# Layer 3's feed-forward weights made inside layer 2's feed-forward loop

## The chip, the cores and the metric

The kernel runs on one core of one Trainium2 chip. The core has five engines with a queue each: TensorE (PE in the profile; its weight loads, PEld, overlap the matmuls), VectorE (DVE), ScalarE (ACT), GpSimd (POOL) and SyncE (SP), which here only issues transfers. An engine works through its queue in order; semaphores tie the queues together. The metric is device microseconds of one launch. Before the change the median of 10 runs is 2324.54 us (2320.92 to 2329.66).

## The reference, cut to what matters

Four layers follow each other on x of shape (4, 256, 256), each a cross attention to a context of 1601 rows and a feed-forward part. The change touches the feed-forward part of layer 2, where each token goes to one of four experts, and that of layer 3, whose weights are first rounded to -1, 0 or 1:

```python
def _quant_weight(w):
    scale = jnp.mean(jnp.abs(w)) + EPS
    wq = jnp.clip(jnp.round(w / scale), -1.0, 1.0)
    return (wq, scale)
...
gate = jax.nn.silu(_qlinear(x, w_gate))
up = _qlinear(x, w_up)
return _qlinear(gate * up, w_down)
```

`_qlinear(x, w)` rounds its input too, multiplies by the rounded weight and scales the product back. The three weights are 256 x 1024 numbers each. Rounded weights and scales depend on nothing but the inputs of the kernel.

Layer 2's feed-forward part is

```python
probs = softmax(x @ Wr + br); top_w, top_idx = top_k(probs, 1)
y = (silu(x @ Wg[e]) * (x @ Wu[e])) @ Wd[e]      # e = top_idx of the token
out = y * top_w
```

and layer 3's attention has 32 heads of 8, with normalised queries and keys.

## The kernel before

**Order.** A framework puts the instructions of each engine in order by a cost model of its own, so a line can run well before or after its place in the program. An instruction given to `pin` keeps the program's order among the pinned ones of its engine. Matmuls made with `mm`, and transposes handed to `ordered`, are pinned while `self.strict` is set. In layer 3's main loop every instruction is pinned.

**Layer 2's feed-forward part** (`l2_ffn`, L992). The router sorts the 1024 tokens by expert into NS = 11 tiles of 128 rows, each tile for one expert. Eleven indirect transfers on POOL's queue (L1154) gather the rows `f2xr`, through three buffers; the first can start when `f2src` is there. The hidden width 1024 is cut into NC = 4 chunks. The loop at L1204 goes over 44 pairs of chunk and tile, in 46 steps s, three stages deep: `gated` (L1173: four matmuls `f2gu`, Silu on ScalarE, product `f2h` on DVE), `turned` (L1182: two transposes `f2tph`, copied by ScalarE to `f2hT`) and `down` (L1190: matmuls `f2y`, added by DVE to `f2acc`). During the first 11 steps `brought` (L1166) transposes the next gathered tile into `f2xsT`, with an eviction by ScalarE and DVE in turn. The profile shows a float32 matmul as two.

**Early work for layer 3.** `l3_early` (L1839) makes keys and values of layer 3's first batch, a tile of 128 context rows at a time: four matmuls into one bank (`f2fill`), two copies by ScalarE, squares and their sums for every two tiles. There are NM = 13 such tiles, and `fill(n)` takes n steps of the generator. Eight steps are taken ahead of the loop (L1068, L1093, L1160), the others in steps 10 to 15 and 39 to 43 (L1209 to L1212). Behind the last tile the generator loads the next batch's context on SP's queue, takes the root of the sums (L1864) and goes through the keys in eight parts: POOL scales a part (L1918) and splits it with DVE (L1968, L1969), DVE transposes it (L1922), SP stores it (L1930, `kd<-kt`).

Behind the loop POOL gathers the results (L1225). Layer 3 starts with 11 tiles of batch 1 (`fill`), between which lie the first batch's normalisation, transposes, the copy `xT` (L2048) and the queries.

**Layer 3** (`l3`, L1985). The main loop at L2334 goes over 4 batches, 4 groups of heads and 13 tiles of keys. A step has eight score matmuls `s`, two exponentials of 128x1024 on ScalarE (`e`), and the matmuls `o` of the step before. After each group DVE copies `o` to `os`. Between steps `slot` (L2287) deals pieces of other streams: keys and values of later batches, queries, and from the second batch on the feed-forward part of the batch before. A piece tells its cost in advance, or asks for the one spare bank of PSUM by `yield True`.

One of these streams is `weights` (L2074), dealt in the first batch only. For each of the three weights it issues two transfers of 512 KB on POOL's queue, sums absolute values with DVE (two of 128x1024), adds the partitions up by a matmul with ones, makes scale and reciprocal, and rounds in three passes of DVE over each half. `half` (L2280), the feed-forward part of a finished batch, waits until all three weights are there.

Of the kernel before, what the change touches and what calls it, by code (L numbers as in the profile page):

```python
# [11 lines left out]
F32 = mybir.dt.float32  # L12
# [85 lines left out]
class Kernel:  # L98
# [893 lines left out]
    def l2_ffn(self, other):  # L992
# [13 lines left out]
        with ExitStack() as es:  # L1006
# [152 lines left out]
            chunks.append(load(1))  # L1159
            fill(3)  # L1160
            self.strict = False
            expert = []
# [3 lines left out]
            def brought(n):  # L1166
                tp = ps.tile([P, 2, P], F32, name="f2tpx", tag="tp")
                for k in range(2):
                    nc.tensor.transpose(tp[:, k, :], xr[n][:, k * P : (k + 1) * P], self.ident)
                self.evac(xsT[:, n], tp)  # L1170
                expert.append(nc.tensor.value_load(ei[:, n : n + 1], min_val=0, max_val=E2 - 1))
# [29 lines left out]
            work = [(c, n) for c in range(NC) for n in range(NS)]  # L1201
            hs, hTs = {}, {}
            brought(0)
            for s in range(len(work) + 2):  # L1204
                if s < len(work):
                    hs[s] = gated(*work[s])
                    if s + 1 < NS:
                        brought(s + 1)
                    elif s < NS + 5:  # L1209
                        fill(1)  # L1210
                    elif s >= len(work) - 5:
                        fill(1)  # L1212
                if 0 <= s - 1 < len(work):
                    hTs[s - 1] = turned(hs.pop(s - 1))
                if s >= 2:
                    down(*work[s - 2], hTs.pop(s - 2))
                    c, n = work[s - 2]
                    if n == NS - 1 and c + 2 < NC:
                        chunks.append(load(c + 2))
            self.back = []  # L1220
            for t in range(8):
# [592 lines left out]
    def values3(self, pool):  # L1814
# [7 lines left out]
        return va  # L1822

    def l3_begin(self, b, st):
        st["kr"] = self.a3.tile([P, NM, D], F32, name="kr3")
# [159 lines left out]
    def l3(self, first):  # L1985
# [10 lines left out]
        with ExitStack() as es:  # L1996
# [7 lines left out]
            self.va3.append(self.values3(self.late3))  # L2004
            wq, ws = {}, {}

# [27 lines left out]
            def queries(b, st, fill=lambda n: None):  # L2034
# [37 lines left out]
                yield 0.0  # L2072

            def weights():  # L2074

                for name, n in (("l3_wg", 2), ("l3_wu", 2), ("l3_wd", 8)):
                    v = i[name].rearrange("(k p) e -> p k e", p=P)
                    w = []
                    for c in range(2):
                        w.append(two.tile([P, I3], F32, name="wf3", tag="g3"))  # L2080
                        nc.gpsimd.dma_start(
                            w[c].rearrange("p (k e) -> p k e", k=n // 2), v[:, c * n // 2 : (c + 1) * n // 2]
                        )
                    for _ in range(2):
                        yield 0.0
                    sm = self.small.tile([P, 2], F32, name="wsum")
                    for c in range(2):
                        yield 1.2
                        nc.vector.tensor_reduce(sm[:, c : c + 1], w[c], AX.X, ALU.add, apply_absolute_value=True)
                    yield 0.0  # L2090
                    yield True
                    tot = bank()[:, 0:2]
                    self.mm(tot, self.ones, sm, True, True)
                    s = one.tile([P, 1], F32, name=name + "s")
                    r = self.small.tile([P, 1], F32, name="wrec")
                    nc.vector.tensor_reduce(s, tot, AX.X, ALU.add)
                    nc.vector.tensor_scalar(s, s, 1.0 / (I3 * D), 1e-5, ALU.mult, ALU.add)
                    nc.vector.reciprocal(r, s)
                    wb = one.tile([P, n, 2048 // n], BF16, name=name + "b")
                    wr = wb.rearrange("p k e -> p (k e)")  # L2100
                    for c in range(2):
                        yield 0.8
                        nc.vector.tensor_scalar(w[c], w[c], r, RND, ALU.mult, ALU.add)
                        yield 0.7
                        nc.vector.tensor_scalar(w[c], w[c], RND, 1.0, ALU.subtract, ALU.min)
                        yield 0.7
                        nc.vector.tensor_scalar(wr[:, c * I3 : (c + 1) * I3], w[c], -1.0, None, ALU.max)
                    wq[name], ws[name] = wb, s
                    yield 0.0

# [376 lines left out]
    def run(self):  # L2487
# [23 lines left out]
        self.l2_xattn()  # L2511
        with ExitStack() as es:
            self.l3_open(es)
            first = {}
# [127 lines left out]
```

## Time and profile before

| | |
|---|---|
| median of 10 runs | 2324.54 us |
| the profiled execution | 2321.94 us, its span 2319.9 us |
| granted TensorE clock, mean | 0.987 |
| layer 2's feed-forward loop, first `f2gu` to last `f2y` | 1673.4 to 1814.3 us |
| layer 3's first exponential; last | 1838.4; 2290.6 us |
| first batch of layer 3, first exponential to the second batch's first | 1838.4 to about 1958.7 us |
| ScalarE's waits for `s` in 1836 to 1960 us | 21.7 us |
| busy share of the span: PE, DVE, ACT, POOL | 96%, 63%, 55%, 41% |

All times inside the program are microseconds from the start of the span of one profiled execution. In a timeline a row has the start, the time it took, the engine, the line, the operation with the tiles written and read, the count, and in brackets how long the engine had been idle and what ended that. In layer 3 all lines are L77, a helper that pins, so rows are told apart by tiles. Buffer numbers are left out of names: `wf` is the tile `wf3`, `f2gu` stands for all of its buffers.

### The profile page before, as it was taken

The page shows a single profiled execution, that of the slowest core. Times are in us where ns is not written, and L with a number is a line of the kernel's source. Part 1 is how long each engine was busy: PE and PEld are TensorE (multiplying, and loading weights), DVE is VectorE, ACT ScalarE, POOL GpSimd, SP SyncE. Part 2 cuts the span into 40 slices and gives each one's busy share as a digit, 9 for nine tenths or more (in the row PEclk, how much of TensorE's full clock was granted, in tenths as well). Part 3 has the DMA queues.
Part 4 walks back from the last instruction along what each step waited for, and adds up shares of the span by engine and source line. Part 5 has one row for each costly group of instructions (what it writes and reads, how often), then busy time and mean ns, then how long its engine had stood idle before and what let it go on. Part 6 is the DMA issues. An engine that isn't in the chain of part 4 may idle for free.

```text
span 2319.9 us, 42336 instructions
## 1 busy us (share of the span) xinstructions
PE 2233.8 (96%) x14379; PEld 1375.8 (59%) x14379; DVE 1467.2 (63%) x3534; ACT 1276.4 (55%) x2884; POOL 953.1 (41%) x1716
## 2 busy tenths in 40 slices
PE   8989999999989999999999999999999989999997
PEld 5677988867745555555555555555765633443332
DVE  5543645953567777887787778777334575748343
ACT  3334546633665555544555555554332587888996
POOL 2014655612445554555445545554221354334220
PEclk9999999989999999999999999999999999999999
DMA  7155687833721111111111111100534453434220
GB/s 275 43 187 167 187 161 211 264 100 98 230 87 40 52 53 53 57 53 36 50 48 53 53 53 53 57 2 10 200 125 121 138 150 107 103 95 110 79 68 18
DMA packets 157166, 234.47 MB, mean 101 GB/s; under 512 B 33993, under 2 KB 122825, under 8 KB 155754
## 3 DMA queue, kind: packets, MB, share of 16 engines
q1 hardware_dynamic: 140902, 190.86, 25.5%
q0 software_dynamic: 11280, 31.60, 5.9%
q10 hardware_dynamic: 4772, 9.31, 1.3%
q8 instruction: 118, 1.93, 0.3%
q14 instruction: 94, 0.77, 0.1%
HBM read 169.94 MB, written 61.74 MB: 100 GB/s over the span
## 4 chain that ended last, share of the span: by engine, by line
PE 82%; DVE 8%; DMA 4%; ACT 2%; issue 2%; POOL 1%; SPq 0%; ACTq 0%; DVEq 0%; POOLq 0%
PE o L117 18%; PE s L117 17%; PE o L77 7%; PE b L77 4%; PE f2gu L117 3%; PE s L77 3%; PE f1gu L117 3%; PE fill L1328 2%; PE acc L117 2%; PE f0gu L117 2%; PE tpq L117 2%; PE av L117 2%; DMA f0xr<-f0xd,f0src 2%; PE f0y L117 2%; PE f2y L117 1%
## 5 line engine op out<-in xcount | busy, mean ns | idle before, releaser
L1593 ACT ACTIVATE p<-s,nmsm 128x448 f32<-128x448 f32 (+2 forms) x512 | 324.7, 639 | 388.0 <-DVE nmsm L1588 315.7
L117 PE MATMUL o<-pT,va 128*128 128x256 f32 (+2 forms) x1920 | 431.2, 377 | 0.8 <-DVE pT L1637 0.3
L117 PE MATMUL s<-kT,qT 128*32 128x448 f32 (+2 forms) x4096 | 423.7, 550 | 4.2 <-ACT p L1593 4.2
L77 ACT ACTIVATE e<-s 128x1024 f32<-128x1024 f32 (+1 forms) x416 | 393.0, 1040 | 51.8 <-PE s L77 50.5
L117 PEld LDWEIGHTS o<-pT,va 128*128 128x128 f32 (+1 forms) x1920 | 344.4, 190 | 124.9 <-issue 72.5
L1631 POOL TENSOR_SCALAR p<-p,rm 128x416 f32<-128x416 f32 x508 | 318.3, 650 | 6.3
L1588 DVE TENSOR_REDUCE nmsm<-s 128x1 f32<-128x448 f32 (+4 forms) x384 | 292.8, 783 | 4.2
L1637 DVE STREAM_TRANSPOSE pT<-p 128x448 f32<-128x448 f32 (+4 forms) x384 | 277.8, 777 | 10.3 <-POOL p L1631 10.3
L117 PEld LDWEIGHTS s<-kT,qT 128*32 128x32 f32 x4096 | 121.7, 109 | 249.7 <-issue 213.1
L77 PE MATMUL o<-e,va 128*32 128x512 f32 (+1 forms) x1664 | 247.8, 609 | 5.2 <-DVE os L77 5.1
L1621 POOL TENSOR_TENSOR rm<-em,tot 32x8 f32<-32x8 f32 x256 | 50.3, 196 | 336.3 <-DVE tot L1618 304.0
L1585 DVE TENSOR_TENSOR s<-s,mask 128x64 f32<-128x64 f32 (+4 forms) x384 | 92.2, 259 | 123.8 <-PE s L117 77.8
L77 PEld LDWEIGHTS s<-qb,kb 32*128 32x128 f32 (+1 forms) x1664 | 64.8, 179 | 175.3 <-issue 130.8
L526 POOL DMA_INDIRECT f0xr<-f0xd,f0src x95 | 91.8, 966 | 58.8 <-PE f0tph L583 47.8
L77 PE MATMUL s<-qb,kb 32*128 32x256 f32 (+1 forms) x1664 | 110.3, 329 | 4.0 <-ACT e L77 1.3
L1328 PE MATMUL fill<-wkc_early,ctxT 128*128 128x256 f32 (+1 forms) x444 | 107.6, 393 | 6.7 <-ACT va_early L1336 4.5
L1593 ACT ACTIVATION_READ_ACCUMULATOR p<-s,nmsm 128x1 f32 x512 | 100.5, 196 | 0.0
L77 POOL CAST kb<-kf 128x384 fp32r<-128x384 f32 (+1 forms) x126 | 64.8, 543 | 86.7 <-PE s L77 35.2
L1328 PEld LDWEIGHTS fill<-wkc_early,ctxT 128*128 128x128 f32 (+1 forms) x444 | 85.1, 195 | 22.0 <-ACT va_early L1336 5.6
L117 PE MATMUL f2gu<-f2wgu,f2xsT 128*128 x176 | 84.7, 605 | 0.6 <-ACT f2xsT L114 0.3
L634 POOL DMA_INDIRECT f0yt<-f0yd,f0slot x64 | 68.1, 1064 | 35.0 <-DMA kd<-kT_early 15.8
L77 PEld LDWEIGHTS o<-e,va 128*32 128x32 f32 (+1 forms) x1664 | 41.4, 108 | 68.7 <-issue 35.1
(565 smaller groups left out, 3661.6 us busy)
## 6 DMA issues: line engine op xcount, KB each, us to landing
kf<-kd SPq DMA_DIRECT2D x384, 48.0 KB
vd<-va_early SPq DMA_DIRECT2D x96, 128.0 KB
kd<-kT_early SPq DMA_DIRECT2D x48, 256.0 KB
kT<-kd SPq DMA_DIRECT2D x16, 768.0 KB
va<-vd SPq DMA_DIRECT2D x16, 768.0 KB
kd<-kt SPq DMA_DIRECT2D x96, 128.0 KB
f0yd<-f0ys SPq DMA_DIRECT2D x95, 128.0 KB
ctxT<-in_ctxT SPq DMA_DIRECT2D x5, 1664.0 KB
```

The lines of the kernel that those rows point to most:

```text
L77: ins = f(*a, **kw)
L117: self.ordered(self.nc.tensor.matmul(out, lhsT, rhs, start=start, stop=stop, **kw))
L526: nc.gpsimd.indirect_dma_start(out=t, out_offset=None, in_=xd[:, :], in_offset=bass.IndirectOffsetOnAxis(ap=src[:, n : n + 1], axis=0),)
L634: nc.gpsimd.indirect_dma_start(out=yt, out_offset=None, in_=yd[:, :], in_offset=bass.IndirectOffsetOnAxis(ap=slot[:, t, r : r + 1], axis=0),)
L1328: ins = nc.tensor.matmul(tp[:rows, t, :], ctxT[u // NKV2][:, k, c0 : c0 + rows], w[u % NKV2][:, k, :], start=k == 0, stop=k == 1,)
L1585: nc.vector.tensor_tensor(sv, sv, mask[:, e0:e1, : nt - CT, :].rearrange("p n t i -> p n (t i)"), ALU.add)
L1588: nc.vector.tensor_reduce(ms[:, 0, e0:e1], s[:, n0:n1, : nt * 32], AX.X, ALU.max, negate=True)
L1593: nc.scalar.activation(p[:, n, : nt * 32], s[:, n, : nt * 32], AF.Exp, bias=ms[:, 0, e : e + 1], accum_out=ms[:, 1, e : e + 1],)
L1621: nc.gpsimd.tensor_tensor(r[32 * a : 32 * a + 32], e[:, a], tot, ALU.mult)
L1631: nc.gpsimd.tensor_scalar(p[:, n, : nt * 32], p[:, n, : nt * 32], r[:, e : e + 1], 1.0, ALU.mult, ALU.mult)
L1637: self.pin(nc.vector.transpose(pT[:, 2 * c + n0 : 2 * c + n1, :nt, :].rearrange("p n t i -> p n (t i)"), p[:, n0:n1, : nt * 32],))
```

## The change

`weights` leaves layer 3 and becomes `l3_weights`, a generator called in layer 2's feed-forward loop at the end of each step from step 10 on, and run out behind the loop. The sums of absolute values become activations on ScalarE, four of 128x512 for each weight, and the roundings go to GpSimd. Its instructions on ScalarE, DVE and GpSimd are pinned. Rounded weights and scales lie in a pool of their own, open until the end of layer 3, the loaded weights in a pool of layer 2's part. `half` no longer waits for weights.

Apart from that, `fill(3)` ahead of the loop becomes `fill(4)`, one further `fill(1)` lies behind the first `brought`, the order of PE stays pinned until step 1, the transposes of `brought` are pinned as long as that holds, and the first batch's `xT` is copied by ScalarE.

```diff
-            fill(3)
-            self.strict = False
+            fill(4)
...
+            wf = es.enter_context(tc.tile_pool(name="f2wf", bufs=2))
+            small = self.l3_weights(wf, self.take)
             brought(0)
+            fill(1)
             for s in range(len(work) + 2):
+                if s == 1:
+                    self.strict = False
...
+                if s >= 10:
+                    next(small, None)
+            for _ in small:
+                pass
...
+    def l3_weights(self, pool, bank):
+        nc = self.nc
+        self.wb3, self.ws3 = {}, {}
+        self.w3 = self.es3.enter_context(self.tc.tile_pool(name="w3", bufs=1, side="right"))
+        for name, n in (("l3_wg", 2), ("l3_wu", 2), ("l3_wd", 8)):
+            v = self.i[name].rearrange("(k p) e -> p k e", p=P)
+            w = []
+            for c in range(2):
+                w.append(pool.tile([P, I3], F32, name="wf3", bufs=2))
+                nc.gpsimd.dma_start(w[c].rearrange("p (k e) -> p k e", k=n // 2), v[:, c * n // 2 : (c + 1) * n // 2])
+            for _ in range(3):
+                yield
+            sm = pool.tile([P, 4], F32, name="wsum", bufs=1)
+            for c in range(4):
+                junk = pool.tile([P, 512], F32, name="wjunk", bufs=1)
+                h = slice(c % 2 * 512, c % 2 * 512 + 512)
+                self.pin(nc.scalar.activation(junk, w[c // 2][:, h], AF.Abs, accum_out=sm[:, c : c + 1]))
+                yield
+            yield
+            tot = bank()[:, 0:4]
+            self.ordered(nc.tensor.matmul(tot, self.ones, sm, start=True, stop=True))
+            s = self.ws3[name] = self.w3.tile([P, 1], F32, name=name + "s")
+            r = self.small.tile([P, 1], F32, name="wrec")
+            self.pin(nc.vector.tensor_reduce(s, tot, AX.X, ALU.add))
+            self.pin(nc.vector.tensor_scalar(s, s, 1.0 / (I3 * D), 1e-5, ALU.mult, ALU.add))
+            self.pin(nc.vector.reciprocal(r, s))
+            wb = self.wb3[name] = self.w3.tile([P, n, 2048 // n], BF16, name=name + "b")
+            wr = wb.rearrange("p k e -> p (k e)")
+            for c in range(2):
+                yield
+                self.pin(nc.gpsimd.tensor_scalar(w[c], w[c], r, RND, ALU.mult, ALU.add))
+                yield
+                self.pin(nc.gpsimd.tensor_scalar(w[c], w[c], RND, 1.0, ALU.subtract, ALU.min))
+                self.pin(nc.gpsimd.tensor_scalar(wr[:, c * I3 : (c + 1) * I3], w[c], -1.0, None, ALU.max))
...
-            wq, ws = {}, {}
+            wq, ws = self.wb3, self.ws3
...
-                nc.vector.tensor_copy(xT, tp.rearrange("p k q t -> p k (q t)"))
+                (nc.vector.tensor_copy if b else nc.scalar.copy)(xT, tp.rearrange("p k q t -> p k (q t)"))
...
-            def weights():
...
-                while len(wq) < 3 or "xn" not in states[b]:
+                while "xn" not in states[b]:
...
-                    streams = [t for t in streams if t.left] if b else [Stream(weights(), 3)]
+                    streams = [t for t in streams if t.left] if b else []
```

More of the change, by code (lines that the diff above doesn't have):

```diff
@@ L1168, in brought @@
                 for k in range(2):
-                    nc.tensor.transpose(tp[:, k, :], xr[n][:, k * P : (k + 1) * P], self.ident)
+                    self.ordered(nc.tensor.transpose(tp[:, k, :], xr[n][:, k * P : (k + 1) * P], self.ident))
                 self.evac(xsT[:, n], tp)
@@ L2072, in queries @@
                 yield 0.0
-            def weights():
[L2076 to L2109, printed above, removed]
             def scale_of(v, name):
@@ L2512, in run @@
         with ExitStack() as es:
+            self.es3 = es
             self.l3_open(es)
```

## The prediction

> **What bounds the kernel now.** I read the page first (TensorE, "PE", is busy 96% of the span), then the table of windows over layer 2's feed-forward loop (1673 to 1815 us) and the start of layer 3 (1838 to 1965 us), then the timeline of the places where a window sags. Columns of a window: its length, busy time and count of PE, weight load, DVE, ACT and POOL, granted clock, DMA share, GB/s.
>
> ```profile
> 1665.00:1673.00 8.00, 4.02 (x18) 2.70 (x16) 1.37 (x2) 2.77 (x8) 3.35 (x5) 0.84 0.93 381
> 1673.00:1683.00 10.00, 9.44 (x26) 4.88 (x26) 2.02 (x5) 2.06 (x6) 2.67 (x3) 0.78 0.15 43
> 1750.00:1770.00 20.00, 20.00 (x73) 12.19 (x73) 8.91 (x18) 4.76 (x15) 2.09 (x2) 1.00 0.70 217
> 1845.00:1900.00 55.00, 49.56 (x416) 18.43 (x416) 46.61 (x108) 44.91 (x50) 25.71 (x34) 0.94 0.57 167
> ```
>
> In the loop PE is full and POOL nearly empty. In layer 3's first 55 us DVE, which makes the weights there, is the fullest after PE (85%), and the clock dips to 0.94. At the loop's start the timeline shows PE waiting for the gathers, and then a slow clock:
>
> ```profile
> 1670.49 0.66 PE L1169 MATMUL f2tpx<-ident,f2xr 128*128 128x128 f32 x2 [2.67 <-DMA f2xr<-f2xd,f2src]
> 1672.46 0.66 PE L1169 MATMUL f2tpx<-ident,f2xr 128*128 128x128 f32 x2 [1.31 <-DMA f2xr<-f2xd,f2src]
> 1673.38 5.63 PE L117 MATMUL f2gu<-f2wgu,f2xsT 128*128 x8 [0.26 <-issue]
> ...
> 1705.72 1.89 PE L117 MATMUL f2fill<-wkv,ctx 128*128 128x256 f32 x8
> ```
>
> Eight f2gu matmuls take 5.63 us; four take 1.88 later. The last line is an early tile inside the loop. A step without one looks like this; f2gu starts repeat every 2.80 us, and ACT and DVE wait for PE:
>
> ```profile
> 1763.58 0.38 ACT L1178 ACTIVATE f2h<-f2gu 128x256 f32<-128x256 f32 x1 [2.15 <-PE f2gu L117]
> 1763.87 0.37 ACT L1187 COPY f2hT<-f2tph 128x256 f32<-128x256 f32 x1
> 1764.10 0.38 DVE L1179 TENSOR_TENSOR f2h<-f2h,f2gu 128x256 f32<-128x256 f32 x1
> 1764.47 1.88 PE L117 MATMUL f2gu<-f2wgu,f2xsT 128*128 x4
> 1766.18 0.38 PE L1185 MATMUL f2tph<-ident,f2h 128*128 128x128 f32 x2
> ```
>
> In layer 3 the pace is ScalarE's exponentials, two per tile of keys: 18 in 16.51 us, 1.83 us a pair, when nothing is late. Two places where the weights make something late:
>
> ```profile
> 1866.10 1.56 DVE L77 TENSOR_SCALAR l_wgb<-wf 128x1024 bf16<-128x1024 f32 x1
> 1869.37 0.68 DVE L77 COPY os<-o 128x512 f32<-128x512 f32 x1
> 1870.11 1.94 PE L77 MATMUL o<-e,va 128*32 128x512 f32 x8 [2.61 <-DVE os L77]
> 1872.87 1.94 ACT L77 ACTIVATE e<-s 128x1024 f32<-128x1024 f32 x2 [3.34 <-PE s L77]
> ```
>
> ```profile
> 1889.03 0.38 PE L77 MATMUL b<-wsum,ones 128*128 128x2 f32 x2 [1.83 <-DVE wsum L77]
> 1890.94 1.94 ACT L77 ACTIVATE e<-s 128x1024 f32<-128x1024 f32 x2 [1.63 <-PE s L77]
> ```
>
> **Part 1, early tiles.** There are 13. Before, 8 lie ahead of the loop and 5 in it (steps 10 to 14). After, 9 lie ahead of the first gather's transposes, a tenth behind them, and 3 in the loop (steps 10 to 12). A tile in the loop stretches a step from 2.80 to 4.53 us, so two fewer give -2 x 1.73 = **-3.5 us**. Their new places: the first fits the 2.67 us wait, ending near 1669.6, ahead of the gather (1670.5). The second starts behind the transposes at 1671.15 and ends near 1672.9, where f2gu began at 1673.38. In the order now pinned, the second gather is transposed behind f2gu 0: 1672.9 + 1.73 + 0.38, then some 0.7 for its eviction (0.37 to 0.42 plus hand-over), so f2gu 1 starts near 1675.8 and f2gu 2 near 1678.4, against 1679.74: **-1.3 us**, at full clock. Whether the clock holds is open: after idle stretches of 2.67 and 1.31 us it was 0.50, after 3.05 us (at 1740) it stayed 1.00. With gaps under 1 us I take it to hold. If not, the 1.9 us (5.63 - 2 x 1.88) come back: +0.6. The best bound, no bubble for f2gu 1, is -2.0.
>
> The end of the early work (square root of the sums, two context loads of 1664 KB on the SP queue, first key scaling) moves from step 15 to 13. The loads stand behind the chunk's loads as before, and are first needed at 1814.
>
> **Part 2, the weights in the loop.** The generator takes 12 calls per matrix, 36 in steps 10 to 45, its last two roundings behind the loop.
> ScalarE: 12 sums of 128x512. The nearest row, a square of 128x512, is 0.64, an accumulator read 0.20: 0.84 each, 10 us in all. A step leaves ScalarE 2.15 us idle. Even ahead of the Silu it is hidden: f2h is ready at 1764.5 for a transpose at 1766.18, a slack of 1.7.
> The Trainium skill ("ScalarE: Activation LUTs", Table sets) lists abs as a filler of every table set; no run here shows an Abs. By that the load rival below is worth 0.
> TensorE: three sums over partitions; their row in layer 3 is 0.38: **+1.1 us**, as the loop is PE's.
> DVE: nine instructions of some 0.15, hidden unless they wait for the sum's matmul; the Silu product is queued behind them.
> POOL: 18 roundings of 128x1024. Rows of the same operation:
>
> ```profile
> L1631 POOL TENSOR_SCALAR p<-p,rm 128x448 f32<-128x448 f32 x254 | 158.0, 643 | 0.0
> L259 POOL TENSOR_SCALAR mfb<-mfb 128x1601 f32<-128x1601 f32 x4 | 7.7, 1914 | 0.3
> ```
>
> The four of 128x1601 have a median of 1.54, so 0.64 + 576 x 0.77 ns = 1.09 us each (1.28 by their mean, which holds one slow case of 3.05): 20 us, with six DMA issues of 0.6 to 0.8 another 4. POOL idles 36.6 us before its key scaling and has 16 us of that; 40 of 100 us. The last group can start when its scale is there (step 42, near 1802) and needs 6.5 us, before the eight gathers behind the loop (1812). If it is late, 12 us of early tiles cover it: rows are normalised by 1824.7 for transposes at 1826.96.
> Each matrix (1 MB, on POOL's queue) has three steps, 8.4 us, before its first sum; in layer 3 the last took 5.0 us from issue to its first half used, at a DMA share near 0.8. Later than that would block ScalarE, and the Silu behind.
> What can cost is POOL's order. The key scaling and splitting of layer 3's first keys run in the same steps, and DVE's key transposes wait for POOL:
>
> ```profile
> 1731.81 5.40 POOL L1918 TENSOR_TENSOR kr<-kr,ss 128x512 f32<-128x512 f32 x5 [36.56 <-DVE ss L126]
> 1738.46 1.25 DVE L1922 STREAM_TRANSPOSE kt<-half 128x1024 f32<-128x1024 f32 x1 [4.25 <-POOL half L1969]
> 1740.06 0.44 PE L1185 MATMUL f2tph<-ident,f2h 128*128 128x128 f32 x2 [3.05 <-DVE f2h L1179]
> ```
>
> The Silu product stands behind that transpose, so PE waited 3.05, and 0.64 a step on. A rounding ahead of a split adds 1.09, against a slack of 1.7. Bounds: -3 (the old stall goes, since scaling starts earlier) to +9 (three more such stalls). I take **+1**, near the lower end, as half the transposes will be done before rounding begins in step 19.
> The Trainium skill ("SBUF — State Buffer", Two separate sides) speaks against the move: GpSimd and a DVE operation in a two-port mode lock each other out for a whole instruction. The trace agrees: DVE's split of 128x512 took 1.28 beside POOL and 0.41 alone. By it a few splits cost 0.9 more each; by the loop's row (0.38 to 0.42 whether POOL works or not) the Silu product, which PE waits for, costs nothing more.
>
> **Part 3, layer 3's first batch without them.** DVE loses 6 sums of 1.2, 12 passes of 0.68 to 1.4, 6 of 0.65 to 1.66, some 25 us in 1847 to 1965; POOL loses the six issues; PE three sums. What of it was on the path is read from ScalarE's waits: 3.34 at 1872.87 down to some 0.4 (-2.9); the two waits behind it at half clock, 1.28 and 1.43, partly the query product (-1.0); 1.63 at 1890.94, where PE waited for a weight sum (-1.6); 0.80 at 1903, the same output copy behind a rounding (-0.8); 1.53 at 1917.8, keys behind stores that waited for DVE and shared the DMA with the last matrix (half, -0.8); 1.49 at 1953.7, a DVE shuffle behind a rounding (-0.9). Sum -8.0. Elsewhere in these 120 us a product of keys costs ScalarE 0.56 whoever shares DVE, and no weights change that. New dealing of the streams will bring its own waits; I take **-7**, bounds -3 (only the first wait goes) and -11 (all 21 us of ScalarE's waits halve).
>
> **Entry.** The first xT copy moves to ScalarE (0.60 for 0.69), which has evictions to do then; an early tile of 1.73 covers it. 0, +-1.
>
> **Sum**: -3.5 - 1.3 + 1.1 + 1 - 7 = -9.7 us, on a profiled run of 2321.9 (span 2319.9). That run lies 2.6 under the median 2324.5, so the median becomes **2314.8**. A measurement of this kernel can tell 0.2%, 4.6 us, from no change.
>
> **Rivals.**
> (a) The exponentials pace layer 3 anyway, or the freed slots are filled with other DVE work at once: part 3 gives 0. For: ScalarE has no idle at all in 1852 to 1864 although DVE is full. Against: the waits above name the copy and the sum. -2.7: 2321.8.
> (b) POOL's roundings hold up DVE's key transposes, and PE with them. For: the 3.05 us stall. Against: POOL's 40% load and the slack of 1.7. If six transposes stall like the old one: 6 x 3.05 = 18 instead of 1, net +7.6: 2332. It decides from 10.7 us of new stalls on.
> (c) Each Abs between two Silus brings two table loads of 1.28: 0.38 + 0.37 + 0.84 + 2.57 = 4.16 for a step of 2.80, 12 x 1.36 = +16: 2331. Against: squares sit between Silus in the trace with no load.
> (d) The weights arrive late or their tiles hold up layer 3's first ones by place: a few us, inside the range.
>
> **How the numbers follow.** Forecast 0.74, (a) 0.14, (b) 0.09, (c) 0.03. Best ends: -3.5 - 2.0 + 1.1 - 3 - 11 = -18.4: 2306. Bad ends of the forecast: -3.5 + 0.6 + 1.1 + 9 - 3 = +4: 2329. All of either at once is unlikely, so the range is 2307 to 2326; it leaves out (b) and (c); the forecast's own is 2308 to 2319. Faster 0.75 (forecast, a little of (a)), same 0.13, slower 0.12.
>
> **What would show it.** Right: f2gu 0 to 3 at 1.88 us from the start, three f2fill tiles in the loop, steps of 2.80, no ACT_TABLE_LOAD beside Abs, no wait of 3 us at the first output copy, first batch some 113 instead of 120 us. Wrong: f2tph waiting for DVE behind key transposes in steps 19 to 36; f2h waiting for a sum; gathers behind roundings; the same 21 us of ScalarE waits in the first batch.

## The result, and the profile after

The changed kernel takes **2348.43 us**, median of 12 runs (2338.56 to 2358.7), the kernel before 2323.8, median of 40 runs beside it: a ratio of 1.0106, 95% interval 1.0094 to 1.0118. It is 24.6 us slower, where 9.7 less were forecast. The profiled execution took 2356.17 us, its span 2354.5; of the 34.6 us between the spans, 5.7 were there already at the last addition of layer 2's attention, ahead of everything that is changed, and 0.8 lie behind layer 3's last exponential. The 5.7 are spread from execution to execution: this one lies 7.7 us above the median.

From there on the two profiles can be laid side by side in four stretches. A: that addition to the first `f2gu`. B: to the end of the last `f2y`. C: to layer 3's first exponential. D: to the end of its last exponential. Starts and ends are read from the timelines, in us.

| | A | B | C | D |
|---|---|---|---|---|
| before | 29.8 | 140.9 | 24.1 | 452.2 |
| after | 37.3 | 149.0 | 32.6 | 456.2 |
| difference (sum 28.0) | +7.4 | +8.1 | +8.5 | +4.0 |
| the prediction's terms | -1.3 | -3.5 + 1.1 + 1 | 0 | -7 |

Every stretch went the wrong way. (The -1.3 was counted to the third `f2gu`, so a part of it belongs to B.) The windows of after that answer to those shown of before, moved by the delay of the place, with one behind the loop as the fourth (columns as before: length, PE, weight load, DVE, ACT, POOL, clock, DMA share, GB/s):

```profile
1670.70:1678.70 8.00, 6.21 (x29) 5.13 (x27) 1.37 (x2) 3.65 (x10) 4.00 (x5) 1.00 0.98 408
1678.70:1688.70 10.00, 6.21 (x14) 4.04 (x15) 0.69 (x1) 1.55 (x4) 0.99 (x1) 0.66 0.27 98
1755.70:1775.70 20.00, 14.32 (x45) 8.61 (x45) 6.51 (x12) 3.15 (x10) 14.98 (x9) 0.83 0.59 196
1836.00:1860.00 24.00, 18.07 (x74) 15.24 (x75) 4.72 (x12) 8.69 (x23) 20.57 (x19) 0.86 0.30 88
1875.00:1930.00 55.00, 51.20 (x444) 18.61 (x437) 38.64 (x98) 47.54 (x53) 27.26 (x41) 0.97 0.58 167
```

In the second row, where the loop would have started, PE has 6.2 of 10 us at a clock of 0.66. In the loop (third) PE, which had been full, has 14.3 of 20, and POOL, which had 2.1, has 15.0. The fourth is the stretch behind the loop: PE has 18.1 and POOL 20.6 of 24. The same stretch before:

```profile
1814.50:1838.50 24.00, 22.63 (x112) 19.41 (x112) 11.89 (x29) 13.52 (x34) 10.57 (x15) 1.00 0.36 106
```

Only the last row, layer 3's start, looks as forecast: DVE 38.6 for 46.6, clock 0.97 for 0.94.

**Stretch A**, in the timeline of after (start, time, engine, line, operation; in brackets the idle time ahead and what ended it):

```profile
1670.54 0.63 POOL L1842 DMA_DIRECT2D wf<-in_l_wg  x1 [19.86 <-DVE f2src L1136]
1671.47 1.04 POOL L1154 DMA_INDIRECT f2xr<-f2xd,f2src  x1 [0.30 <-issue]
...
1675.03 0.59 POOL L1842 DMA_DIRECT2D wf<-in_l_wg  x1
...
1680.94 0.41 PE L1168 MATMUL f2tpx<-ident,f2xr 128*128 128x128 f32 x2 [4.02 <-DMA f2xr<-f2xd,f2src]
...
1682.91 3.75 PE L117 MATMUL f2fill<-wkv,ctx 128*128 128x256 f32 x8 [1.56 <-PEq L1170]
...
1686.45 2.77 PE L117 MATMUL f2gu<-f2wgu,f2xsT 128*128 x4
```

The weights' first two transfers are not issued in step 10, where the program has them, but ahead of the first gather and of the fourth. The change pins the engines' work on the weights, not the transfers, and the framework moved them to the first place that their tiles allow. The first gathered tile is used 9.5 us after its issue, while PE has run out of early tiles. Before it was 7.0, from this issue to the transposes at 1670.49:

```profile
1663.50 1.05 POOL L1154 DMA_INDIRECT f2xr<-f2xd,f2src  x1 [0.22 <-issue]
```

The early tile behind the transposes takes 3.75 instead of 1.73, at a slow clock. Not all of A is the change's: from the addition to `f2src`, ahead of every gather, 20.7 us pass after and 19.0 before, and 19.0 to 22.1 in all profiles, so 1.7 of the 7.4 is spread. From `f2src` to the first `f2gu` it is 16.5 for 10.8.

**Stretch B.** The groups of `wf` (count; minimum, median and maximum in ns; first and last start; the third is the first matrix's) and the worst of the stalls:

```profile
L1863 POOL TENSOR_SCALAR wf<-wf,wrec x6: 1111/1120/1123, 1751.8 to 1839.2; 128x1024 f32<-128x1024 f32 x6
L1865 POOL TENSOR_SCALAR wf<-wf x6: 3638/3653/3669, 1753.0 to 1840.4; 128x1024 f32<-128x1024 f32 x6
L1866 POOL TENSOR_SCALAR l_wgb<-wf x2: 2780/2781/2782, 1756.8 to 1766.1; 128x1024 bf16<-128x1024 f32 x2
```

```profile
1761.27 3.66 POOL L1865 TENSOR_SCALAR wf<-wf 128x1024 f32<-128x1024 f32 x1
1764.87 1.28 POOL L2013 TENSOR_TENSOR half<-kr,half 128x512 f32<-128x512 f32 x1
1766.18 1.25 DVE L1966 STREAM_TRANSPOSE kt<-half 128x1024 f32<-128x1024 f32 x1 [6.37 <-POOL half L2013]
1767.46 1.71 DVE L2012 TENSOR_SCALAR half<-kr 128x512 uint32<-128x512 uint32 x1
1769.09 0.40 DVE L1178 TENSOR_TENSOR f2h<-f2h,f2gu 128x256 f32<-128x256 f32 x1
1769.55 0.69 PE L1184 MATMUL f2tph<-ident,f2h 128*128 128x128 f32 x2 [5.68 <-DVE f2h L1178]
1771.74 2.79 PE L117 MATMUL f2gu<-f2wgu,f2xsT 128*128 x4
```

The first pass costs what was priced (1.12 for 1.09), the second 3.65, the third 2.78: 7.55 us a half instead of 3.3, 45.3 in all instead of 20. Read from the top: a split of keys stands behind a pass of 3.66; DVE's key transpose waits for the split, the product `f2h` stands behind the transpose, and PE waits 5.7 us for it, with a slow clock behind (2.79 for 1.88). PE waits for `f2h` three times, 2.0, 5.7 and 2.5 us; before, 3.05 and 0.64. The 2.0 at 1742 come ahead of the first rounding (1751.8), and e1, e2 and e9 have them too; the other two stand behind a pass of 3.66.

**Stretch C**, at the loop's end:

```profile
1831.53 1.11 POOL L1863 TENSOR_SCALAR wf<-wf,wrec 128x1024 f32<-128x1024 f32 x1 [18.00 <-issue]
...
1844.14 2.78 POOL L1866 TENSOR_SCALAR l_wdb<-wf 128x1024 bf16<-128x1024 f32 x1
1846.95 0.37 ACT L1899 COPY va<-fill 128x256 f32<-128x256 f32 x1 [8.42 <-POOL l_wdb L1866]
...
1847.38 9.47 PE L117 MATMUL fill<-wkv,ctx 128*128 128x256 f32 x32 [5.93 <-ACT va L1899]
...
1848.32 1.10 POOL L1233 DMA_INDIRECT f2yt<-f2yd,f2slot  x1 [0.17 <-issue]
```

The last matrix's roundings begin 4 us before the loop ends, since its sum reaches DVE only at 1830.8, and take 15.4. Two things wait: the eight gathers in POOL's queue, and the first copy into the second batch's values `va`. With that copy the early tiles, which the prediction had named as the cover, stand still for 5.9 us and then start slowly (32 matmuls in 9.47, at a clock of 0.50 from 1847 to 1852; 24 took 5.45 before the wait). Before, the tiles ran through:

```profile
1814.77 12.35 PE L117 MATMUL fill<-wkv,ctx 128*128 128x256 f32 x56 [0.51 <-DVE f2acc L1197]
```

**Stretch D.** The wait of 3.34 at the first output copy is gone, but one of 3.59 has come ahead of it, and others in the later batches:

```profile
1892.66 1.22 DVE L77 STREAM_TRANSPOSE kt<-half 128x1024 f32<-128x1024 f32 x1
1892.91 1.00 PE L77 MATMUL b<-ident,xn 128*128 128x128 f32 x4 [1.94 <-DVE row L77]
...
1896.60 3.75 ACT L77 ACTIVATE e<-s 128x1024 f32<-128x1024 f32 x4 [3.59 <-PE s L77]
...
1902.55 0.69 DVE L77 COPY os<-o 128x512 f32<-128x512 f32 x1 [1.44 <-PE o L77]
...
1989.65 1.94 PE L77 MATMUL o<-e,va 128*32 128x512 f32 x8 [2.43 <-DVE os L77]
...
1992.41 1.94 ACT L77 ACTIVATE e<-s 128x1024 f32<-128x1024 f32 x2 [3.11 <-PE s L77]
```

At the 23rd exponential PE waits for DVE's `row`, and ScalarE 3.59 us. The first output copy, at 1902.55, is then on time: from 1901.6 to 1921 ScalarE waits for nothing. The second batch has a new wait of 3.11 at an output copy, the third one of 3.06. ScalarE's waits for `s` in the first 104 exponentials, one batch, are 19.0 us (before 21.1), in the next 104 19.8 (15.6). From one batch's first exponential to the next one's, the first batch takes 117.4 us (before 120.3), the second 123.3 (118.0) and the third 114.6 (113.1). So the first batch gains 2.9 us, and the two behind it lose 6.8.

### The profile page after: what moved, and what is told of

Same layout as the page of the kernel before. It is cut to its first block, busy times and chain, and to the rows that moved or that the text cites. A ratio compares the mean times of both kernels' runs of the same rounds, so it can differ in the third digit from the quotient of the medians.

```text
span 2354.5 us, 42356 instructions
## 1 busy us (share of the span) xinstructions
PE 2256.5 (96%) x14379; PEld 1388.0 (59%) x14379; DVE 1442.3 (61%) x3509; ACT 1283.9 (55%) x2909; POOL 996.1 (42%) x1734
## 4 chain that ended last, share of the span: by engine, by line
PE 78%; DVE 8%; POOL 4%; DMA 4%; issue 3%; ACT 3%; SPq 0%; ACTq 0%; PEldq 0%; DVEq 0%; POOLq 0%
PE o L117 18%; PE s L117 17%; PE o L77 8%; PE b L77 4%; PE s L77 3%; PE f1gu L117 3%; PE f0gu L117 2%; PE acc L117 2%; PE f2gu L117 2%; PE tpq L117 2%; PE av L117 2%; PE fill L1336 2%; DMA f0xr<-f0xd,f0src 2%; PE f0y L117 2%; PE f1y L117 1%
```

## The experiments

Theory: (1) transfers ahead of the gathers cost stretch A; (2) GpSimd's price for two of the passes costs B and C; (3) layer 3 loses what it gains, as its other pieces are dealt into the places that came free. Rivals stand in the expectations. The runs stood beside a kernel before of 2325.4 (e1 to e4) and 2323.5 us (e5 to e8), later beside one of 2372.3 (e9 to e12) and 2373.5 (e13 to e16), where the unchanged part ahead of stretch A was some 40 us longer in every profile, why is not known; so ratios are compared there. C without any weight work is 24.1 in the first eight and 26.1 in the others. A varies by up to 3 us ahead of `f2src`, as said above.

| run | ratio to before | 95% | A | B | C | D |
|---|---|---|---|---|---|---|
| e1 roundings on DVE | 1.0022 | 1.0010-1.0035 | 37.3 | 135.9 | 24.2 | 455.5 |
| e2 gathers first | 1.0025 | 1.0012-1.0038 | 30.6 | 137.3 | 32.5 | 455.9 |
| e3 tiles only | 0.9985 | 0.9974-0.9996 | 32.6 | 136.3 | 24.1 | 453.9 |
| e4 no weight work | 1.0012 | 1.0001-1.0023 | 34.5 | 135.2 | 24.1 | 453.1 |
| e5 gathers first, DVE | 0.9990 | 0.9978-1.0003 | 32.1 | 135.8 | 24.2 | 455.3 |
| e6 as e4, same deal | 0.9957 | 0.9944-0.9970 | 33.8 | 136.2 | 24.1 | 442.1 |
| e7 last matrix on DVE | 1.0076 | 1.0061-1.0091 | 37.3 | 147.0 | 24.2 | 455.4 |
| e9 fast forms | 1.0002 | 0.9991-1.0013 | 37.1 | 136.4 | 26.2 | 453.2 |
| e10 DVE, gathers first, same deal | 0.9931 | 0.9916-0.9945 | 32.0 | 135.8 | 26.3 | 441.9 |
| e11 fast, gathers first, same deal | 0.9934 | 0.9920-0.9948 | 32.9 | 136.8 | 26.2 | 441.7 |
| e12 as e6, costs alone | 0.9985 | 0.9973-0.9998 | 33.9 | 135.4 | 26.1 | 451.1 |
| e13 after, same deal | 1.0027 | 1.0015-1.0039 | 36.4 | 146.9 | 34.7 | 441.1 |
| e14 as e6, turns alone | 0.9988 | 0.9978-0.9997 | 34.0 | 135.4 | 26.1 | 450.8 |
| e15 fast, gathers first, share 12 | 0.9970 | 0.9958-0.9982 | 30.6 | 135.8 | 26.3 | 453.1 |
| e16 before, share 12 | 1.0029 | 1.0019-1.0040 | 31.0 | 140.8 | 26.4 | 462.5 |

**e1, roundings on VectorE.** All three passes:

```diff
-                self.pin(nc.gpsimd.tensor_scalar(w[c], w[c], r, RND, ALU.mult, ALU.add))
+                self.pin(nc.vector.tensor_scalar(w[c], w[c], r, RND, ALU.mult, ALU.add))
```

> The 18 roundings go back to VectorE, in the same places of layer 2's loop; all else as in the changed kernel (median 2348.4 us, 24.6 over the kernel before). Theory (GpSimd's slow clipping passes hold up the key splits in the loop and the gathers and the ones of layer 3's values behind it): the loop's three stalls of some 6, 2 and 2.5 us with their slow clock go (some -10), and so does the late end of the loop's work (-8): 2328 to 2332 us; what is left over the kernel before is the late start of the loop (+7). Rival (VectorE is then as late with its product f2h as it was behind the splits, since 18 roundings of 0.7 to 1.4 us, some 17 us, stand ahead of it): under 6 us gained, 2342 to 2348. Rival (the excess lies in layer 3 and at the loop's start): no change, 2348.

2330.4 us. B loses 13.1 and C 8.4; A and D stay. Theory (2) holds, and DVE's own 18 passes hold up little: the waits of 5.7 and 2.5 are gone, and B is 0.7 above the 135.2 without weight work.

**e2, gathers first.**

```diff
-                nc.gpsimd.indirect_dma_start(
+                self.pin(nc.gpsimd.indirect_dma_start(
...
-                nc.gpsimd.dma_start(w[c].rearrange(...), v[...])
+                self.pin(nc.gpsimd.dma_start(w[c].rearrange(...), v[...]))
```

> All eleven gathers of layer 2's loop and the six weight transfers are pinned on GpSimd's queue, so that the first two weight transfers (512 KB each) are issued behind the gathers instead of ahead of the first and the fourth; all else as in the changed kernel. Theory (those two transfers fill the DMA engines and GpSimd's queue, so that the first gathered tile is 3 us late and the clock drops): the first f2gu falls from 37 to 28 or 30 us behind the last addition of the router's part, and the kernel gains 7 to 9 us: 2340 us. Rival (the clock and the gathers were late in that execution by chance, or are late because the chunk's load shares the DMA engines anyway): under 2 us, 2347 or more.

2331.5 us: A falls by 6.7, as expected, but B by 11.8 as well, which was not. The timeline of e2 shows the loop's start:

```profile
1666.07 1.05 POOL L1154 DMA_INDIRECT f2xr<-f2xd,f2src  x1 [18.65 <-DVE f2src L1136]
...
1672.83 0.41 PE L1168 MATMUL f2tpx<-ident,f2xr 128*128 128x128 f32 x2 [0.80 <-ACT va L1899]
...
1674.71 1.97 PE L117 MATMUL f2fill<-wkv,ctx 128*128 128x256 f32 x8 [1.47 <-DMA f2wgu<-in_l_wgu]
...
1676.51 1.88 PE L117 MATMUL f2gu<-f2wgu,f2xsT 128*128 x4
```

The first gather is used 6.8 us after its issue, no longer waited for, and the clock holds. For B the order of POOL's queue gives the reason: with the pins, two of the key splits come ahead of the second pass that they stood behind in the changed kernel. The slow passes are there, and PE's longest wait for `f2h` in the loop is one of 2.03 us in the early steps. So the loop's stalls need both, a long pass and a split queued behind it. C keeps its 32.5. Between the five runs with the gathers first (A 30.6 to 32.9) and the five with the transfers ahead of them (36.4 to 37.3, after among them) lie 5.5 us by their means; counted from `f2src`, without the unchanged part, it is 4.5 (16.2 for 11.6).

**e3, the tiles alone**, in the kernel before: `fill(4)`, the `fill(1)` behind `brought(0)`, the pins until step 1.

> The kernel before with the early tiles of the change alone (a fourth tile ahead of the first gather's transposes, a fifth behind them, order pinned until step 1); the weights stay in layer 3. The forecast's first term: two early tiles fewer in the loop (-3.5) and the second gather's wait filled (-1.3): 2319 us. Rival (the early tiles are only moved, as PE waits for the gathers as long as before, and the clock still drops at the loop's start): -1.5 to 0, 2322 to 2324. Rival (the pinned order makes later gathers wait behind f2gu at half clock): +2, 2326.

2320.36 us beside 2325.41, and the ratio with its interval makes -3.5 us (-0.9 to -6.0). From the third `f2gu` to the loop's end the profile gives 3.8 us (130.8 for 134.5), near the 3.5 priced for two tiles. From `f2src` to the third `f2gu` it takes 0.5 more (17.7 for 17.2), where 1.3 less were forecast:

```profile
1668.97 0.41 PE L1168 MATMUL f2tpx<-ident,f2xr 128*128 128x128 f32 x2 [0.71 <-ACT va L1857]
1670.85 2.78 PE L117 MATMUL f2fill<-wkv,ctx 128*128 128x256 f32 x8 [1.47 <-DMA f2xr<-f2xd,f2src]
1673.42 2.80 PE L117 MATMUL f2gu<-f2wgu,f2xsT 128*128 x4
```

Between the transposes and the second tile PE idles 1.47 us. The row names the next gathered rows as what ended it, but all 15 runs with the new order have 1.3 to 1.6 us there, and six of them name PE's own queue at L1170, which loads the number of the tile's expert; so the rows are probably not the cause. The eight matmuls of the tile take 2.78 instead of 1.73, and `f2gu` 2.80 instead of 1.88. In e2 the same gap of 1.47 left the tile at 1.97. The prediction's "Whether the clock holds" goes either way, and the windows show in what the two runs differ. The traces give the clock in periods of 3.41 us; two of e3, then two of e2:

```profile
1668.43:1671.85 3.42, 1.42 (x7) 1.14 (x8) 0.04 (x1) 0.89 (x3) 0.95 (x1) 1.00 0.58 223
1671.85:1675.26 3.41, 3.41 (x8) 2.02 (x7) 0.39 (x1) 1.17 (x3) 0.00 (x0) 0.50 0.00 0
```

```profile
1669.72:1673.14 3.42, 2.62 (x13) 1.90 (x11) 0.69 (x1) 1.82 (x5) 0.00 (x0) 1.00 0.95 382
1673.14:1676.55 3.41, 1.94 (x10) 1.66 (x10) 0.00 (x0) 0.37 (x1) 0.95 (x1) 1.00 0.67 254
```

In e3 both gaps, 0.7 and 1.47, fall into one period, PE has 1.42 of it, and the next period is at 0.50. In e2 they fall into two, with 2.62 and 1.94, and the clock stays whole. The kernel before fits: ahead of its slow clock PE had 0.74 of a period (1667.08 to 1670.49), while the gap of 3.05 at 1740 is divided between two (1.66 and 2.11).

**e4, no weight work.** `l3_weights` only fills the rounded weights and scales with constants.

> The changed kernel with the weights' transfers, sums and roundings left out (the rounded weights are set to 1 and the scales to 0.01 by GpSimd): the early tiles of the change, and layer 3's first batch without weights. By the forecast's terms it gains -3.5 - 1.3 - 7, 2312 us; by rival (a) of the prediction (layer 3's first batch is paced by the exponentials, and what is freed is filled at once) 2319; if layer 3 without the weights in its first batch is even slower, because keys are dealt earlier and output copies wait behind them, 2323 or more. The difference between this kernel and the changed one is what the weight work costs in its new place: 36 us by the first, 25 by the last.

2327.0 us, the third of the three outcomes. With no transfers, sums or roundings anywhere, the kernel is 6.6 us slower than e3, which has all of them in layer 3. Some 2 of that are its own, as one fill of 1.80 us stands ahead of the first gather in POOL's queue, and its profile is 3.8 longer behind layer 3's last exponential (32.7 for 28.9), so D says more than the total. D is 453.1: part 3, priced at -7, is worth nothing as the pieces are dealt.

**e5, both repairs**, e1's edit and e2's.

> Both of the first two edits: gathers ahead of the weight transfers, and the roundings on VectorE. If the costs lie in separate stretches and add up stage by stage (start of the loop 30.5 us behind the router's last addition, as with the gathers first; loop 136 and loop's end to the first exponential 24.2, as with VectorE; layer 3 455.5, as in all three), it stands at the kernel before + 0.7 - 5 + 0 + 3.3 = -1: 2323 to 2325 us. Rival (the two edits cured the same stalls in the loop, and VectorE's roundings bring their own): no better than either alone, 2329 to 2331.

2321.49 us, 2.0 under before, the interval touching no change. They add up, since A, B and C are separate stretches; D's 455.3 takes back 3.1 of the 5.1 that B gives, and A 2.2.

**e6, the old dealing.** In e4, an empty stream takes the weights' places in the first batch:

```diff
-                    streams = [t for t in streams if t.left] if b else []
+                    streams = [t for t in streams if t.left] if b else [Stream(ghost(), 3)]
...
+            def ghost():
+                for _ in range(3):
+                    for cost in (0.0, 0.0, 1.2, 1.2, 0.0, True, 0.8, 0.7, 0.7, 0.8, 0.7, 0.7, 0.0):
+                        yield cost
```

> The kernel without weight work (transfers, sums and roundings left out, rounded weights 1, scales 0.01), but in layer 3's first batch an empty stream takes the places that the weights' pieces took (the same costs told in advance, the same turns at the spare bank, no instruction), so that keys, values and queries of later batches are dealt as before the change. Theory (what the weights' absence saves in the first batch is given back because those pieces are dealt earlier and meet the output copies at ends of groups): layer 3 falls by 3 to 6 us, 2321 to 2324. Rival (the freed VectorE time is worth nothing, whatever the order of the pieces): 2327, layer 3 as long as with the streams dealt anew, 453.

2311.9 us, 11.7 under before, beyond the expectation. D falls to 442.1, from 452.2 with the weights in it and 453.1 without. The rival falls: the freed time is worth 10 us, if nothing else is put in it. ScalarE's waits in the first 104 exponentials are 12.6 us (e4 18.6). The longest waits for `s` that e4 has in the first two batches, the first ten us aside, against the longest of e6 there:

```profile
1866.09 3.75 ACT L77 ACTIVATE e<-s 128x1024 f32<-128x1024 f32 x4 [3.30 <-PE s L77]
...
1961.43 1.94 ACT L77 ACTIVATE e<-s 128x1024 f32<-128x1024 f32 x2 [2.63 <-PE s L77]
```

```profile
1983.51 1.94 ACT L77 ACTIVATE e<-s 128x1024 f32<-128x1024 f32 x2 [1.43 <-PE s L77]
```

**e7, the last matrix's six passes on VectorE**, by the same edit for `l3_wd` alone.

> The changed kernel with only the last matrix's six roundings on VectorE. Theory (that matrix alone holds GpSimd behind the loop and, by it, the gathers and the ones of the second batch's values): loop's end to the first exponential 24 instead of 32.6 us, loop and entry as in the changed kernel: 2340 us. Rival (GpSimd is late anyway, with key splits): 30 us or more there, 2346 to 2348.

2340.1 us, and C 24.2: the last matrix alone made stretch C.

**e8, the forms by themselves.** All layers are left out; three passes of each form over 128x1024.

> All layers are left out; what remains are passes over 128x1024 from one tile to another, three of each form, first on GpSimd and then on VectorE, with no other engine at work: subtract and min, max to bf16, multiply and add, and the single operations. Theory (the clipping forms are slow on GpSimd in themselves): subtract-min 3.65 and max to bf16 2.78 us as in the loop, multiply-add 1.1. Rival (they were slowed in the loop by VectorE's or the DMAs' use of the same memory): all forms 1.1 us alone. My price in the prediction was 1.09 for all.

The groups of e8 by form (busy us, mean ns):

```profile
L2514 POOL TENSOR_SCALAR x_sub_add<-src 128x1024 f32<-128x1024 f32 x3 | 10.9, 3633 | 0.2
L2514 POOL TENSOR_SCALAR x_sub_min<-src 128x1024 f32<-128x1024 f32 x3 | 10.9, 3630 | 0.7 <-DVE r L2508 0.5
L2514 POOL TENSOR_SCALAR x_add_min<-src 128x1024 f32<-128x1024 f32 x3 | 10.9, 3629 | 0.2
...
L2514 POOL TENSOR_SCALAR x_mul_f<-src 128x1024 f32<-128x1024 f32 x3 | 8.3, 2772 | 0.2
...
L2514 POOL TENSOR_SCALAR x_max_b<-src 128x1024 bf16<-128x1024 f32 x3 | 8.3, 2769 | 0.2
...
L2514 POOL TENSOR_SCALAR x_mul_add<-src,r 128x1024 f32<-128x1024 f32 x3 | 3.4, 1121 | 0.2
L2514 POOL TENSOR_SCALAR x_min_max<-src 128x1024 f32<-128x1024 f32 x3 | 3.1, 1041 | 0.2
L2514 DVE TENSOR_SCALAR x_mul_add<-src,r 128x1024 f32<-128x1024 f32 x3 | 2.3, 751 | 0.1
...
L2514 DVE TENSOR_SCALAR x_mul_f<-src 128x1024 f32<-128x1024 f32 x3 | 2.1, 694 | 0.1
```

The times of the loop return within 0.02 us with nothing else running, so it is the form, not contention. But it isn't clipping: min and max in one pass take 1.04, a single multiply 2.77, subtract and add 3.63. Of the forms tried, only two pairs are fast, multiply-add and min-max.

The Trainium skill ("GPSIMD Engine Reference", 4.1 Engine selection) has GpSimd near line rate for operations with one input and about twice VectorE's time for two. The multiply-add pass comes near that (1.12 against VectorE's 0.75 in e8); the single multiply does not (2.77 against 0.69, four times), and the measurement decides.

**e9, fast forms**, in the changed kernel; the order on every queue is unchanged:

```diff
-                self.pin(nc.gpsimd.tensor_scalar(w[c], w[c], RND, 1.0, ALU.subtract, ALU.min))
-                self.pin(nc.gpsimd.tensor_scalar(wr[...], w[c], -1.0, None, ALU.max))
+                self.pin(nc.gpsimd.tensor_scalar(w[c], w[c], 1.0, -RND, ALU.mult, ALU.add))
+                self.pin(nc.gpsimd.tensor_scalar(wr[...], w[c], 1.0, -1.0, ALU.min, ALU.max))
```

> The changed kernel with the two clipping passes in the pairs of operations that GpSimd ran fast by themselves: multiply by 1 and add the negative rounding constant (1.12 us there) for subtract and min (3.63), and min and max in one pass, written as bf16 (1.04 in f32) for max alone (2.77). Same engine, same order of every queue, six groups of 3.3 instead of 7.5 us, 20 us in all, which is what the prediction took. Theory (the price of those passes makes the loop's stalls and the late gathers): loop 136 to 138 instead of 149, loop's end to the first exponential 24 to 26 instead of 32.6, start of the loop still 37, layer 3 still 455: 2328 to 2331 us. Rival (their place in the queue does it, not their length; the key splits wait in any case): over 2338.

Ratio 1.0002, some 24 us under the changed kernel, a little better than expected. The passes take 1.12, 1.05 and 1.04 us, the last in bf16; B is 136.4 (135.2 to 136.2 without weight work), C 26.2, as without weight work in these later runs (26.1). Same engine, same queue order: what is left is price alone. Of PE's waits for `f2h` over 0.8 us one of 2.0 remains. The last matrix's group starts 4.0 us ahead of the loop's end here too, but takes 6.7, and the early tiles cover what lies behind the loop.

**e10 and e11, all repairs**: e5 with e6's stream, and the same with the fast forms on GpSimd.

> Roundings on VectorE, gathers ahead of the weight transfers, and in layer 3's first batch the empty stream in the places of the weights' pieces. If the three repairs add up: e5's 2321.5 less the 15 us by which the empty stream shortened the kernel without weight work (2327.0 to 2311.9), of which layer 3 had 11: 2307 to 2311 us, 12 to 16 under the kernel before. Rival (the empty stream's gain was the kernel's without weight work only, as layer 3's start stands otherwise to its loads when the loop carries weights): 2317 to 2321.

> As the run before it, but with the roundings left on GpSimd in the fast forms. If GpSimd's 20 us are hidden as the prediction took them: equal to the run with VectorE, or 1 to 3 us under it since VectorE keeps the loop's products free: 2306 to 2311 us. Rival (splits still wait behind roundings for 1.1 us each, or the last ones hold the gathers): 2 to 6 us over it, 2312 to 2316.

0.9931 and 0.9934: 16 us under the kernel before, as much as expected, and alike. D keeps its 10 us with the weight work in layer 2. In the right forms GpSimd hides the work as well as VectorE does.

**e12 and e14, which property of the dealing.** The empty stream without its three turns at the spare bank, and with nothing but those.

> The kernel without weight work and with the empty stream, less the stream's three turns at the spare bank, so that it takes only the places told by costs (18 pieces of 0.7 to 1.2). Theory (VectorE's pieces dealt earlier make layer 3 longer; the costs hold them back): as with the whole stream, layer 3 442, 2311 to 2314 us. Rival (the three turns at the bank shift the key products against the groups of heads): layer 3 450 or more, 2320 to 2327. If it lies between, both do.

> The kernel without weight work, with an empty stream that takes only its three turns at the spare bank and no place by costs (the counterpart of e12, whose layer 3 took 451 us, against 453 without and 442 with the whole stream). If the turns are what counts: first batch 115 as without the stream, second batch back to 114 or 115 (from 119 to 122), layer 3 443 to 447, ratio 0.997 to 0.999. If both are needed together: 450 to 453, ratio 1.000 or more.

D 451.1 and 450.8, against 453.1 without and 442.1 with the whole stream. Each gives 2 us of 11. The costs shorten the first batch (110.9 to the second's first exponential; 117.0 without the stream, 111.2 with all of it) and lose it in the second (124.9; 121.8 and 117.0); the turns leave the first at 116.1 and the second at 119.4. It is the combination, and no single piece can be named.

**e13, the changed kernel with the empty stream.**

> The changed kernel as it is, with nothing but the empty stream in layer 3's first batch (as in e6). Theory (the empty stream is worth the 11 us of layer 3 to any of these kernels): layer 3 443 to 446 instead of 456 us, the three other stretches as in the changed kernel: 11 us under it, a ratio to the kernel before of 1.005 to 1.007 instead of 1.0106. Rival (its worth hangs on a start of layer 3 on time): 1.009 or more.

1.0027 instead of 1.0106: 18 us, more than the 11 expected; D 441.1, 15 less. A, B and C stay slow. As much as e2's edit, and it touches neither the weights nor GpSimd.

**e15 and e16, the share**: `K3 = [12, 8, 6]` for `[15, 8, 6]`, with e11's other repairs but no empty stream, and in the kernel before.

> Fast forms on GpSimd and gathers first, no empty stream, but the share of the key products at the spare bank in the first batch 12 instead of 15, so that the other streams get more of the turns. Theory (layer 3's length hangs on how the turns fall, and any fitting share brings back what the empty stream does): layer 3 442 to 448, ratio 0.994 to 0.997. Rival (only the old places do it): 453 to 456, ratio 0.998 to 1.000.

> The kernel before with the same share of 12 instead of 15 and nothing else. Theory (the share of 15 fitted the streams as they were dealt with the weights among them, and any other dealing is longer): 3 to 10 us slower, ratio 1.0015 to 1.0045. Rival (layer 3 is insensitive to the share): within 2 us, ratio 0.999 to 1.001.

e15 says nothing of the share: without the weights' stream, 12 and 15 deal the pieces in the same order. It serves as fast forms and gathers first alone: 0.9970, 8 us behind e11, which is the stream's part. In the kernel before, the same 3 points make D 462.5 instead of 452.2 and the kernel 7 us slower: layer 3's dealing is fitted to what is dealt, and a step aside costs as much as the change was to win.

## Why the prediction was wrong

- **GpSimd's roundings: the step that failed in B and C.** "The four of 128x1601 have a median of 1.54 ... 1.09 us each". Those rows are of multiply-add, the others shown of multiply-multiply, and I used their price for all three passes. The first pass, a multiply-add, cost 1.12; the second and third 3.65 and 2.78. The 20 us were 45.3, and e9 puts some 24 us of the total on that alone. The bounds around it, -3 and +9, were set by how many splits wait, with 1.09 in every one.
- **Rival (b) named the mechanism**, POOL holding up DVE's key transposes and PE with them, at 18 us from six stalls. There were two, of 5.7 and 2.5 with a slow clock behind each, and 12.7 us between B in after and with fast forms. I had given it 0.09 because of a slack of 1.7 us against a rounding of 1.09.
- **The last group** was to start near 1802, 12 ahead of the end of the loop, take 6.5 and be covered by 12 us of early tiles. It started 4 us before the end and took 15.4. The start is a misreading of the place, not the passes' doing: step 42 ends near 1809 in the profile before (its last `f2gu` starts at 1809.28), and with fast forms (e9) the group starts 4.0 us before the end as well. With 6.7 us of work that was covered, with 15.4 not; and the cover stood still itself, as its copies into `va` waited for the last rounding. The two share no tile, so the wait must come from the place of a released one, the new pool's; that is argued, not tested. It was in no term; rival (d), "their tiles hold up layer 3's first ones by place", had it at "a few us" and inside the range. C cost 8.5.
- **The order of the transfers.** That each matrix "has three steps, 8.4 us, before its first sum" took the transfers to be issued in step 10. They are not pinned, and the front of this document says that a line can run well before its place. It cost 4.5 to 5.5 us in A and, by the place of the splits, most of B's stalls (e2).
- **The early tiles**: -4.8 forecast, -3.5 measured (e3). The two tiles out of the loop are right (3.8 for 3.5). The -1.3 at its start came out as +0.5 in e3, where the clock dropped, for which the prediction had +0.6, and, against the same profile of before, as -1.1 in e2, e5, e10 and e15, where it held. What the prediction left out is the 1.3 to 1.6 us between the transposes and the second tile, which it let start at 1671.15, right behind them; "gaps under 1 us" was wrong by that.
- **Layer 3, part 3: the step that failed in D.** -7 with bounds -3 and -11. With the dealing held, D falls by 10 to 11 (e6, e10, e11, e13), at the good end of the bounds; as the change deals, it rises by 0.9 (e4) to 4.0 (after). "New dealing of the streams will bring its own waits; I take -7" mis-sized the second half: it brought 11 to 15 us of them (e4 against e6, after against e13). Rival (a), "the freed slots are filled with other DVE work at once", comes nearest, and it had only 0 to offer.
- **Right**: no table load beside the 12 Abs sums (0.64 and 0.19 each), which hold up nothing; sum matmuls of 0.28; the entry's `xT` copy.

What stays open is why the places by cost and the turns at the bank work only together: no run took a single piece of layer 3 out of its new place.

## What to carry to other kernels

Price an operation by a row with the same operations in it, not one of the same name and size: here one name cost 1.04 to 3.65 us for the same tile. In a schedule dealt by costs, taking work out is a change to all that is dealt with it; hold the places first (an empty stream does it in a few lines) to see what the work was worth, and only then deal anew. And what isn't pinned moves: look where transfers without waits will land in their queue before counting on their place.

## What the runs showed of the hardware that was not expected

- GpSimd's `tensor_scalar` over 128x1024 f32, alone on the chip: 1.12 us for multiply-add, 1.04 for min-max, 2.77 for a single multiply, subtract, min or max, 3.63 for subtract-min, add-min or subtract-add. VectorE takes 0.69 for nearly all of these.
- VectorE's first three passes in e8, subtract-min, ran beside GpSimd's and took 1.20 us each; the ones after that, alone and of other forms (add-min among them), 0.69 to 0.75.
- The same idle gap of 1.47 us on PE, behind one of 0.7 to 0.8, left the clock whole in e2 (eight matmuls in 1.97 us) and not in e3 (2.78). In these two the difference is whether both fell into one of the 3.41 us periods in which the traces give the clock.
